# A layer norm's inverse deviations by a power on GpSimd instead of a root on ScalarE, in a cross-attention and mixture-of-experts block

## The chip, the core and the metric

The kernel runs on one core of a Trainium2 chip, in float32. The metric is the device time of one execution in microseconds. A core has five engines that work side by side, each through its own queue in order: TensorE (PE: matmuls and transposes), VectorE (DVE), ScalarE (ACT), GpSimd (POOL), and SyncE (SP), which here only starts transfers.

## The reference

Tokens are x [4, 1024, 256], the context is [4, 64, 256]. With 16 heads of 64 and 8 experts of width 1024, two experts per token:

```python
def _layernorm(x, axis=-1, eps=1e-05):
    m = jnp.mean(x, axis=axis, keepdims=True)
    v = jnp.var(x, axis=axis, keepdims=True)
    return (x - m) / jnp.sqrt(v + eps)

# cross attention, q = layernorm(x), k = v = context
qh = jnp.einsum('bld,hdk->hblk', q, w_qs)
kh = jnp.einsum('bld,hdk->hblk', k, w_ks)
vh = jnp.einsum('bld,hdk->hblk', v, w_vs)
attn = jax.nn.softmax(jnp.einsum('hblk,hbmk->hblm', qh, kh), axis=-1)
out = jnp.einsum('hblm,hbmk->hblk', attn, vh) * qh
out = out.transpose(1, 2, 0, 3).reshape(q.shape[0], q.shape[1], -1)
x1 = x + jnp.tanh(g_xattn[0]) * (out @ w_proj.T + b_proj)

# routed feed-forward on xt = layernorm(x1), top 2 of 8 experts
logits = jnp.einsum('td,ed->te', xt, gate_w)
w_topk, sel = jax.lax.top_k(logits, 2)
w_topk = jax.nn.softmax(w_topk, axis=-1)
combine = zeros((T, E)).at[arange(T)[:, None], sel].add(w_topk)
h = silu(jnp.einsum('td,edf->tef', xt, w1))
y = jnp.einsum('tef,efd->ted', h, w2)
out = x1 + jnp.tanh(g_ffn[0]) * jnp.einsum('ted,te->td', y, combine)
```

There are two norms. The first ("a") feeds the queries, the second ("b") feeds the router and the experts.

## The kernel before

The 4096 tokens are cut into 8 groups of 512; a group is 4 tiles of 128 tokens, and the rows of group g stay on the chip in `xg[g]` (the trace calls these tiles x, buffers x_90 to x_97).

The main loop runs over the groups g and the tiles t of a group. For each tile, `probabilities` makes the scores (L402, the matmuls sc<-keys,qT), takes their maximum over each head's 64 keys (L411, mx), subtracts it (L413, pr<-sc,mx), takes the exp on ACT (L416), sums (L418, sm) and inverts the sum (L419) on DVE, and multiplies on POOL (L421, pr<-pr,sm). `transpose_probabilities` turns the result with PE (L431, pa<-ident,pr) and copies it to aT on ACT (L432). `attend` multiplies with the values (L446, po) and DVE multiplies the result with the query (L455, qT<-po,qT). `project` is L463 (pp<-wp,qT), and L470 adds it to `xg[g]` on DVE. `queries` makes the next group's queries (L387, pq).

The work on routing is one group pair behind: when two groups are finished, `after` is called once for each following tile. Its step 0 calls `ln_stats` for the pair (name "b..."), step 1 `ln_norm` and `logits` for the first of the two groups, step 2 for the second. So the second norm is made four times. For the last pair this comes after the loop, beside the first experts' matmuls.

`ln_stats` gathers mean and variance of each of 8 tiles on DVE (L273 into st, L276 into mv), then makes rstd, the inverse deviations, 128x8 for the pair, in L278 and L279. `ln_norm` subtracts and multiplies tile by tile on DVE (L296). For the second norm it works in place, on `xg[g]`; PE then transposes the tiles (L300, pt_b), ACT copies them (L305, nT_b), and `logits` multiplies with the router's weights (L485, pl<-nT_b,gw), copies on DVE (L493, lT<-pl) and transposes back (L495, pl_t).

`leave` (L1067) stores the finished rows of a group to the output with a DMA from ACT's queue: out_dram<-x. Since the second norm overwrites those rows in place, a normed tile has to wait for the store of its group.

The experts' work comes in slots of 256 or 384 tokens: SP loads weights and rows (L770 to L824), DVE transposes the rows (L836, xT), PE makes the hidden layer (L862, ph<-xT,w), ACT applies silu (L870, hT<-ph), PE makes the output (L987, py), and POOL adds it to the output rows with an indirect DMA (L958, `scatter`). The first slot's hidden layer begins beside the last attention group, the fourth and last pair's norm lies beside the next slots. The small tensors of a slot's tokens (ids) are worked on by DVE in L947 and L950.

Buffers that matter for the order:

- scores have two PSUM buffers (pool ps2): a new one may be written when the subtraction L413 has read the one before the last;
- all other PSUM results (pa, po, pq, pp, pt, pl, and ph until the attention ends) go round four banks (pool ps1);
- the probabilities pr have two buffers in SBUF (pool soft), each free again when its transposes L431 are done.

The order on each engine is set by the tile framework's scheduler at build time, by its own estimates of each operation's cost, within the data dependencies. `behind_softmax` (around L296 for the second norm, and around the scatter) ties an operation to the newest POOL product L421:

```python
newest[:] = [
    nc.gpsimd.tensor_tensor(pr, pr, sm.unsqueeze(2).to_broadcast([P, H, M]), ALU.mult).ins
]
...
def behind_softmax():
    return tc.issue_after(newest[0]) if newest else nullcontext()
```

ACT holds one set of function tables at a time; a function of another set needs a load (ACT_TABLE_LOAD in the trace, LoadActFuncSet in the built order). The root, the exp and the silu each stand in a set of their own here.

Of the kernel before, what the change touches and what calls it, by code (L numbers as in the profile page):

```python
# [8 lines left out]
F32 = mybir.dt.float32  # L9
I32 = mybir.dt.int32  # L10
AF = mybir.ActivationFunctionType
ALU = mybir.AluOpType
# [3 lines left out]
P = 128  # L16
EPS = 1e-5
# [4 lines left out]
def kernel(  # L22
# [36 lines left out]
    nc = tc.nc  # L59
# [26 lines left out]
    const = ctx.enter_context(tc.tile_pool(name="const", bufs=1))  # L86
# [86 lines left out]
    bias = const.tile([P, D], F32, tag="bias", name="bias")  # L173
# [23 lines left out]
        nc.gpsimd.memset(t, 0.0)  # L197
    eps = const.tile([P, 1], F32, tag="eps", name="eps")
    nc.vector.memset(eps, EPS)

    before = const.tile([P, E, E], F32, tag="before", name="before")
    nc.vector.memset(before, 0.0)
# [65 lines left out]
    def ln_stats(groups, name):  # L268
        n = len(groups) * T
        mv = small.tile([P, n, 2], F32, tag="mv", name=f"mv_{name}")  # L270
        for i in range(n):
            st = small.tile([P, 6], F32, tag="st", name=f"st_{name}_{i}")
            first = nc.vector.bn_stats(st, xg[groups[i // T]][:, i % T, :])  # L273
            if i == 0 and name[0] == "a":
                tc.keep_in_program_order(first)
            nc.vector.bn_aggr(mv[:, i, :], st)  # L276
        rstd = small.tile([P, n, 1], F32, tag="rstd", name=f"rstd_{name}")
        nc.scalar.activation(rstd, mv[:, :, 1:2], AF.Sqrt, bias=eps)  # L278
        nc.vector.reciprocal(rstd, rstd)  # L279
        return {g: (mv[:, k * T : (k + 1) * T], rstd[:, k * T : (k + 1) * T]) for k, g in enumerate(groups)}  # L280

    def ln_norm(g, stats, name):
# [762 lines left out]
    ctxT = transposed_context()  # L1045
    pending_keys = keys(ctxT)
    stats = ln_stats([0], "a0")
    next(pending_keys)
    next(pending_keys)
    next(pending_keys)  # L1050
    ln_norm(0, stats, "a")
    next(pending_keys)
    stats = ln_stats(list(range(1, GB)), "a1")
    pending_values = values(ctxT)

# [17 lines left out]
    def after(g, step):  # L1073

        nonlocal entered
        groups = list(range(g - GB + 1, g + 1))
        if step == 0:
            second.update(ln_stats(groups, f"b{g}"))
        elif step == 1:
            second["logits"] = scores_of([R, E], f"lg_{g}")  # L1080
            ln_norm(groups[0], second, "b")
            logits(groups[0], second["logits"])
        elif step == 2:
            for h in groups[1:]:
                ln_norm(h, second, "b")
                logits(h, second["logits"])
        elif step == 3:
            second["routing"] = route(second["logits"], f"{g}")
        if step >= 4:
            if step == 4:  # L1090
                weigh(groups, second["places"])
            first, last = min(6 * (step - 4), 2 * R), min(6 * (step - 3), 2 * R)
            with behind_softmax():
                for i in range(first, last):
                    enter(groups, second["places"], i // R, [i % R])
            entered += last - first
# [130 lines left out]
```

## Time and profile before

| what | us |
|---|---|
| median of 3 runs | 879.75 (878.24 to 880.04) |
| the profiled execution | 878.31 |
| its span | 876.6 |
| PE busy in it | 846.7 |
| DVE, POOL, ACT busy | 452.0, 260.2, 250.6 |

The mean granted clock of TensorE was 0.995 of full speed. PE is the fullest engine: its busy time is close to the span, and the other engines are half idle or more. A long wait of another engine costs nothing unless a matmul stands behind it, so the waits of PE itself are to be read first, then what ended them, stage by stage.

### The profile page before, as it was taken

How to read it: one execution, taken by the hardware profiler on the slowest of the kernel's cores; microseconds unless marked ns; L12 is line 12 of the kernel's file. 1: busy time of each engine (PE TensorE's matmuls, PEld its weight loads, DVE VectorE, ACT ScalarE, POOL GpSimd, SP SyncE). 2: the span in 40 equal slices, each digit the busy share in tenths (PEclk: the TensorE clock that was granted, in tenths of full speed). 3: DMA queues.
4: the chain of work that ended last, by engine and by line, in shares of the span. 5: the costliest groups of instructions: out<-in, count | busy, mean ns of one | idle time of the engine just before them, and what ended most of it. 6: DMA issues, size and time to landing. Idle time of an engine off the chain costs nothing. (4 is left out here: it accounts for less than half of the span.)

```text
span 876.6 us, 13019 instructions
## 1 busy us (share of the span) xinstructions
PE 846.7 (97%) x4632; PEld 665.1 (76%) x4632; DVE 452.0 (52%) x1073; ACT 250.6 (29%) x391; POOL 260.2 (30%) x207
## 2 busy tenths in 40 slices
PE   6999999999999999799999999999999999999995
PEld 4565858576766758587888887777877999999994
DVE  4366484759665975764138212434434445645430
ACT  2574242433342333442032111112121121221210
POOL 3042212113711272205414622222222323133131
PEclk9999999999999999999999999999999999999998
DMA  9999998001200055136675797756481856788421
GB/s 201 338 341 340 341 344 251 25 1 47 75 25 1 25 169 164 49 78 225 185 204 151 192 242 195 192 140 167 93 231 22 236 134 176 181 241 229 114 25 22
DMA packets 163254, 140.56 MB, mean 160 GB/s; under 512 B 72944, under 2 KB 157296, under 8 KB 159344
## 3 DMA queue, kind: packets, MB, share of 16 engines
q1 hardware_dynamic: 143728, 117.84, 46.2%
q0 software_dynamic: 12864, 16.86, 9.9%
q10 hardware_dynamic: 6592, 4.98, 1.8%
q8 instruction: 38, 0.62, 0.3%
q14 instruction: 32, 0.26, 0.1%
HBM read 80.76 MB, written 59.41 MB: 160 GB/s over the span
## 5 line engine op out<-in xcount | busy, mean ns | idle before, releaser
L862 PE MATMUL ph<-xT,w 128*128 128x256 f32 (+1 forms) x960 | 241.9, 408 | 0.1
L862 PEld LDWEIGHTS ph<-xT,w 128*128 128x128 f32 x960 | 180.4, 190 | 50.3 <-issue 1.2
L958 POOL DMA_INDIRECT out_dram<-x,ids x68 | 111.8, 1644 | 312.9 <-DVE x L918 188.1
L870 ACT ACTIVATE hT<-ph 128x1024 f32<-128x1024 f32 (+2 forms) x80 | 71.0, 896 | 271.2 <-PE ph L862 254.2
L421 POOL TENSOR_TENSOR pr<-pr,sm 128x1024 f32<-128x1024 f32 x32 | 61.4, 1918 | 232.4 <-DVE sm L419 169.3
L387 PE MATMUL pq<-nT_a,wq 128*128 128x512 f32 x256 | 116.0, 597 | 7.1 <-DVE qT L455 5.1
L463 PE MATMUL pp<-wp,qT 128*128 128x256 f32 x512 | 113.1, 379 | 0.0
L463 PEld LDWEIGHTS pp<-wp,qT 128*128 128x128 f32 x512 | 97.1, 190 | 18.2 <-issue 5.7
L987 PE MATMUL py<-w,hT 128*128 128x256 f32 x480 | 107.0, 379 | 0.0
L987 PEld LDWEIGHTS py<-w,hT 128*128 128x128 f32 x480 | 90.4, 190 | 12.1
L387 PEld LDWEIGHTS pq<-nT_a,wq 128*128 128x128 f32 x256 | 46.2, 190 | 59.8 <-issue 44.5
L583 POOL DMA_INDIRECT table<-x,to_row x64 | 62.6, 979 | 42.3 <-DVE x L572 21.2
L402 PEld LDWEIGHTS sc<-keys,qT 128*128 128x128 f32 x512 | 62.5, 192 | 11.8 <-issue 11.3
L402 PE MATMUL sc<-keys,qT 128*128 128x128 f32 x512 | 67.0, 278 | 0.0
L432 ACT COPY aT<-pa 128x512 f32<-128x512 f32 x64 | 34.5, 591 | 81.9 <-PE pa L431 71.9
L971 DVE TENSOR_SCALAR x<-py,ids 128x256 f32<-128x256 f32 x30 | 14.5, 482 | 79.4 <-PE py L987 79.3
L908 PE MATMUL q<-sw,sh 128*128 128x128 f32 x456 | 54.0, 275 | 0.0
L411 DVE TENSOR_REDUCE mx<-sc 128x16 f32<-128x1024 f32 x32 | 39.0, 1220 | 26.6 <-PE sc L402 26.4
L908 PEld LDWEIGHTS q<-sw,sh 128*128 128x128 f32 x456 | 52.5, 192 | 0.3
L418 DVE TENSOR_REDUCE sm<-pr 128x16 f32<-128x1024 f32 x32 | 39.0, 1217 | 19.8 <-ACT pr L416 19.8
L394 ACT COPY qT<-pq 128x512 f32<-128x512 f32 x64 | 36.2, 581 | 34.3 <-PE pq L387 34.3
L895 DVE TENSOR_TENSOR sh<-hT 128x512 f32<-128x512 f32 x30 | 20.5, 686 | 48.2 <-ACT hT L870 48.2
(198 smaller groups left out, 873.1 us busy)
## 6 DMA issues: line engine op xcount, KB each, us to landing
w<-in_L_ffn_w_dram SPq DMA_DIRECT2D x60, 1024.0 KB, 6.5
table<-empty SPq DMA_DIRECT2D x8, 4620.0 KB, 36.5
x<-table SPq DMA_DIRECT2D x120, 64.0 KB, 4.5
out_dram<-x ACTq DMA_DIRECT2D x8, 512.0 KB, 7.6
x<-in_x_dram SPq DMA_DIRECT2D x7, 512.0 KB, 9.3
out_dram<-x,ids POOLq DMA_INDIRECT x68, 4.9
wq<-in_L_xattn_w_qs_dram SPq DMA_DIRECT2D x4, 256.0 KB, 5.9
wv<-in_L_xattn_w_vs_dram SPq DMA_DIRECT2D x2, 512.0 KB, 5.9
```

The source lines that it names most:

```text
L387: nc.tensor.matmul(pq, wq[:, c, p * P : (p + 1) * P], nT[g][:, c, :], start=(c == 0), stop=(c == NC - 1),)
L402: nc.tensor.matmul(sc[:, p // 2, :, p % 2, :], of_pair(qT, p)[:, t * P : (t + 1) * P], kT[g // GB][:, p, :], start=True, stop=True,)
L411: nc.vector.tensor_reduce(mx, scv, AX.X, ALU.max)
L418: nc.vector.tensor_reduce(sm, pr, AX.X, ALU.add)
L421: nc.gpsimd.tensor_tensor(pr, pr, sm.unsqueeze(2).to_broadcast([P, H, M]), ALU.mult).ins
L463: nc.tensor.matmul(pp[:, i, :], of_pair(qT, p)[:, t * P : (t + 1) * P], wp[:, p, :], start=(p == 0), stop=(p == NP - 1),)
L583: nc.gpsimd.indirect_dma_start(out=table.rearrange("r (u w) -> (r u) w", w=2), out_offset=bass.IndirectOffsetOnAxis(ap=to_row[:, k, i : i ...
L862: nc.tensor.matmul(ph[:, i, :], a[:, c, f * P : (f + 1) * P], xT[:, c, :], start=(c == 0), stop=(c == NC - 1),)
L870: nc.scalar.activation(hT[f0 // per_tile][:, f1 : f1 + step, :], ph, AF.Silu)
L908: nc.tensor.matmul(to, left[:, f, :], right[:, f, :], start=not onto and f == 0, stop=f == NF // 2 - 1, skip_group_check=onto,)
L958: rows_added = nc.gpsimd.indirect_dma_start(out=outf[:n], out_offset=bass.IndirectOffsetOnAxis(ap=of_rows[:, t, 0, 1:2], axis=0), in_=y[:, t],
L987: nc.tensor.matmul(py[t], hT[f // per_tile][:, f % per_tile, t * P : (t + 1) * P], b[:, f, :], start=(f == 0), stop=(f == NF - 1),)
```

## The change

In `ln_stats`, the second norm no longer takes the root of variance plus eps on ACT and its reciprocal on DVE. It adds eps on DVE and raises the sum to the power −0.5 on POOL, with the exponent from a constant tile broadcast over the 8 columns. The first norm (names that begin with "a") keeps root and reciprocal. Everything behind `rstd` is written as before; what the scheduler does with the new operations is left to it.

```diff
     eps = const.tile([P, 1], F32, tag="eps", name="eps")
     nc.vector.memset(eps, EPS)
+    power = const.tile([P, 1], F32, tag="power", name="power")
+    nc.vector.memset(power, -0.5)
...
         rstd = small.tile([P, n, 1], F32, tag="rstd", name=f"rstd_{name}")
-        nc.scalar.activation(rstd, mv[:, :, 1:2], AF.Sqrt, bias=eps)
-        nc.vector.reciprocal(rstd, rstd)
+        if name[0] == "a":
+            nc.scalar.activation(rstd, mv[:, :, 1:2], AF.Sqrt, bias=eps)
+            nc.vector.reciprocal(rstd, rstd)
+        else:
+            nc.vector.tensor_scalar(rstd, mv[:, :, 1:2], EPS, None, ALU.add)
+            nc.gpsimd.tensor_tensor(rstd, rstd, power.unsqueeze(2).to_broadcast([P, n, 1]), ALU.pow)
         return {g: (mv[:, k * T : (k + 1) * T], rstd[:, k * T : (k + 1) * T]) for k, g in enumerate(groups)}
```

The built order of the changed kernel differs from the one before on these engines (the order itself is a property of the program, not of a run). POOL has the four powers, each directly ahead of the first product L421 of the next tile in the first three places, and between scatters in the fourth. ACT has 10 instructions fewer: four roots and six table loads. On DVE, in the first three places, the first normed tile stands between the maximum L411 and the subtraction L413 of that tile's scores, and the last one of the eight behind the reciprocal L419 of the probability sums in the first two. In the third place the order beside the last attention group also changes: on DVE all eight normed tiles, the index operations L947 and L950, the next maximum L411, the sum L418, the next subtraction L413 and then the reciprocal L419; further on the stream transpose L836 earlier, the third sum L418 ahead of the last four products L455, and the fourth maximum L411 ahead of the copy L493. On PE five of the eight score products of the last tile (each is two matmuls in the trace) stand ahead of the first transposes L431 of that group. In the fourth place the stream transpose L836 stands behind four normed tiles. SP's order is unchanged.

## Prediction

> **What bounds the kernel now.** I read the page first: span, then section 1.
>
> ```profile
> span 876.6 us, 13019 instructions
> PE 846.7 (97%) x4632; PEld 665.1 (76%) x4632; DVE 452.0 (52%) x1073; ACT 250.6 (29%) x391; POOL 260.2 (30%) x207
> ```
>
> PE idles 876.6 − 846.7 = 29.9 us; only what starts a matmul earlier or later counts. The profiled execution took 878.31 us, 1.7 around its span; the median of the runs is 879.75, 1.4 more than it. Next the waits of PE (total, times, longest), and the line view of the root:
>
> ```profile
> PE pa L431 <- POOL pr L421: 5.3, 2, 4.5
> PE pq L387 <- DVE qT L455: 5.1, 6, 1.7
> L278 ACT ACT_TABLE_LOAD  x8: 1283/1283/1283, 3.0 to 443.2; - x8
> L278 ACT ACTIVATE rstd_b<-mv_b,eps x4: 300/300/301, 159.2 to 444.5; 128x8 f32<-128x8 f32 x4
> ```
>
> The second norm is made four times, at 159, 253, 347 and 446 us (stages 1 to 4 below). No wait of PE names it, but one of 4.5 us for the scaled probabilities stands in stage 3. The timeline there (start, us, engine, work, idle before):
>
> ```profile
> 345.61 1.23 DVE L413 TENSOR_TENSOR pr<-sc,mx 128x1024 f32<-128x1024 f32 x1
> 347.67 1.38 DVE L296 TENSOR_SCALAR x<-x,mv_b,rstd_b 128x256 f32<-128x256 f32 x4
> 348.41 3.73 PE L402 MATMUL sc<-keys,qT 128*128 128x128 f32 x32
> 351.04 1.06 DVE L296 TENSOR_SCALAR x<-x,mv_b,rstd_b 128x256 f32<-128x256 f32 x3 [1.98 <-DMA out_dram<-x]
> 352.01 1.21 DVE L418 TENSOR_REDUCE sm<-pr 128x16 f32<-128x1024 f32 x1
> 354.27 0.24 DVE L419 RECIPROCAL sm<-sm 128x16 f32<-128x16 f32 x1
> 354.69 1.90 POOL L421 TENSOR_TENSOR pr<-pr,sm 128x1024 f32<-128x1024 f32 x1 [12.21 <-DVE sm L419]
> ```
>
> The normed tiles overwrite rows that a store (L1067, issued at 343.28) is still reading. DVE therefore stands until 351.04, and the sum, the reciprocal and POOL's product stand behind it; PE's transposes start at 356.64. So a DMA, not the root or its table loads, ends last in stage 3. The stall also costs clock, in the windows view (PE busy is the second column, the granted clock follows POOL):
>
> ```profile
> 352.20:356.60 4.40, 0.00 (x0) 0.00 (x0) 4.40 (x5) 2.15 (x2) 1.90 (x1) 0.98 0.00 0
> 356.60:359.80 3.20, 3.16 (x16) 1.87 (x16) 1.64 (x3) 1.34 (x3) 0.00 (x0) 0.50 0.00 0
> ```
>
> Stage 1's timeline (stage 2 is the same within 0.1 us):
>
> ```profile
> 156.42 1.23 DVE L411 TENSOR_REDUCE mx<-sc 128x16 f32<-128x1024 f32 x1
> 160.85 1.06 ACT L416 ACTIVATE pr<-pr 128x1024 f32<-128x1024 f32 x1
> 163.95 1.90 POOL L421 TENSOR_TENSOR pr<-pr,sm 128x1024 f32<-128x1024 f32 x1 [11.56 <-DVE sm L419]
> 163.96 1.95 PE L402 MATMUL sc<-keys,qT 128*128 128x128 f32 x16
> 165.90 0.33 PE L431 MATMUL pa<-ident,pr 128*128 128x128 f32 x1
> ```
>
> POOL's product ends at 165.85, the scores at 165.9: the transposes start without a wait, with nothing to spare.
>
> **Removed.** Four roots of 0.30 us and, in the built order, six table loads of 1.28 (two each in stages 1, 2 and 4; in stage 3 the silu and exp sets now alternate and the count stays): 1.2 + 7.7 = 8.9 us of ACT, and four DVE reciprocals of 0.20. ACT is busy 29% and ends last nowhere here, so by itself this is worth 0. The Trainium skill, "ScalarE: Activation LUTs", section "What ACT_TABLE_LOAD costs", gives 2.66 us for a switch with its drain; the rows show the root 0.01 us behind its load. Either price lies off PE's path, and the sum is the same.
>
> **Added.** One memset on DVE, under PE's first 4.35 us wait: 0. Four additions on DVE of 128x8, about 0.2 us like the reciprocals they replace: 0. Four powers of 128x8 on POOL, of a length d that no row shows. The nearest rows from below are POOL's copy of 128x4 (0.18 us), from above its product of 128x1024 (1.92) and an indirect store (1.64). A power is many operations on few elements; I take d = 1.0, nearer neither end, and keep 0.2 and 1.9. A loop over single elements could pass the upper end; that is a rival.
>
> **Moved.** In stages 1 to 3 the first normed tile now stands between the maximum and the subtraction on DVE, so DVE waits there for the power, and subtraction, exp, sum, reciprocal and POOL's product queue behind it.
>
> Stage 1, worked out: the addition ends at 156.6, POOL starts 0.17 later (as it does after a reciprocal), so the first tile starts at the later of 157.7 (maximum done) and 156.85 + d. From there: tile 0.33, subtraction 1.14, five tiles 1.63, sum 1.13, tile 0.33, then reciprocal to product 0.42 and product 1.90, together 6.9. With d = 1.0 the product ends at 164.7 instead of 165.85: exp is no longer behind 2.9 us of ACT work, but PE has scores until 165.9. Worth 0. It ends later than 165.9 only if d exceeds 2.1. Stage 2 the same. The store that x_91 waits for is no cover lost: DMA share falls to 0.07 at 158 to 159.
>
> Stage 3: the tiles before the store take 344.75 + d + 2.45 = 348.2, under the wait until 351.04 for any d up to 3.8. Behind 351.04 the new order has four tiles instead of three (1.30), two small index operations (0.14), the second maximum (1.13), the sum (1.13), the second subtraction (1.14), then the reciprocal: at 355.9, against 354.27. Product from 356.3 to 358.2, transposes at 358.25 instead of 356.64: +1.6. In exchange 10 of the 16 matmuls of the fourth scores now stand ahead of the transposes; they need the buffer that the second subtraction frees, at 356.0, and take 2.15 us at half clock, so they fit in the wait. From 356.0 the slow 3.2 us are over at 359.2, the transposes at 359.7, and the third subtraction starts at 359.85 (358.70 before).
>
> What follows is DVE's pace, since `po` and `pt_b` wait for banks that L455 frees: subtraction 1.14, sum 1.13, product 0.59, reciprocal 0.17, three products 1.73, and now a third sum (1.13) where a stream transpose (0.63) stood; the next products start at 365.75 (364.09). The first transposes of the normed rows follow the first of them, at 366.4 (364.80). The work moved forward pays some back, but then the fourth maximum (1.13) stands ahead of the copy lT (L493), which used to come first: scores done at 368.45, maximum to 369.6, copy, `pl_t` at 369.95, and the hidden layer's matmuls at 370.05 instead of 368.55: +1.5. From there on PE is full (its listed waits add up to under 2 us) and nothing gives it back.
>
> Whether PE is slow again after 3.9 us of idleness lies between two rows: 1.72 us at 314 left the clock at 1.00, 4.50 brought it to 0.50. I take the second, being nearer. "TensorE: Matmul & The Clock Gate" (section "Part 1: The HAM clock gate") puts the idle window at about 3.4 us, free-running, which agrees. At full clock the third subtraction would start 0.5 earlier and the sum would be +1.0.
>
> Stage 4: addition at 443.8, power behind scatters that ended at 434; tiles at 444.1 + d, wanted by PE at 452.14: 0 up to d = 6.7. What queues behind the power on POOL starts at 452.
>
> Sum: 0 + 0 + 1.5 + 0 = +1.5, 879.8 for the profiled execution, 881.25 from the median. Its own range is 879.5 to 882.5: +0.9 to +1.9 for the steps, and 0.9 for the spread of the runs.
>
> **Rivals.** First, the slow power (slower): the place is DVE's wait in stages 1 and 2, and it decides from d = 2.1. Each us beyond costs 2 us, one more above 3.8 (stage 3). d = 4 gives +1.5 + 3.8 + 0.2 = 5.5, 885.2; d = 10 would give +27 with stage 4. For it: 8 elements may not be what sets its length. Against: POOL's small rows take 0.1 to 0.3.
>
> Second, the store lands early (faster or level). If it landed by 348.1, as its moving in stages 1 and 2 within 3 us suggests, the second maximum would wait only for its scores at 350.3, and the third subtraction would start at 357.05, 2.8 earlier than in my sum: −1.3, 878.4; with the idle waits around it gone as well, 877.5. Against: the store shares the DMA engines with weight and row loads whose place the change leaves alone (it landed 7.7 us after its issue in stage 3, 7.5 in stage 4).
>
> Third, the new stage 3 order costs nothing visible: the two late chains meet ACT or PE work I have put too early, and 0 remains, 879.75.
>
> **How the numbers follow.** A measurement of this kernel can tell about 0.2% (1.76 us) from no change. My forecast lies just inside, so it is split: chance 0.57, of which 0.33 within and 0.24 slower by more. Slow power 0.25, slower. Early store 0.13, counted as faster though its price is near the bound. No cost 0.05, within. Together faster 0.13, same 0.38, slower 0.49. The range drops the upper part of the slow power (d above 4.5) and the deepest gain: 877.8 to 886.5.
>
> **What would show it.** In the changed profile: the power's row on POOL at 0.2 to 2 us, the first tile's wait for POOL in stages 1 and 2 under 1.3 us, and `pa` at 165.9 and 259.8 without a wait. In stage 3: DVE released by the store at 351.0, the product at 356.3, `pa` at 358.3 behind ten score matmuls at clock 0.50, and a PE wait of about 1.3 us for lT ahead of `pl_t`, which the trace of before has only in the next group (0.41). Wrong: a power over 2.1 us, a release by something other than the store, or the hidden layer's matmuls before 369.5.

## The result and the profile after

The changed kernel took 880.59 us (median of 22 runs, 879.74 to 881.69); in the same series the kernel before took 879.28 (878.24 to 880.60). The ratio is 1.0014, 95% interval 1.0007 to 1.0020: +1.31 us, with an interval of 0.6 to 1.8, inside the 0.2% that was called no difference and slower in sign. The forecast was +1.5, the predicted time 881.2. The profiled execution took 880.54 us around a span of 878.8.

The page after, span and section 1, then the line view of the power (ns minimum/median/maximum, first and last start):

```profile
span 878.8 us, 13010 instructions
PE 846.3 (96%) x4632; PEld 665.7 (76%) x4632; DVE 450.3 (51%) x1074; ACT 242.3 (28%) x381; POOL 266.3 (30%) x211
```

```profile
L285 POOL TENSOR_TENSOR rstd_b<-rstd_b,power x4: 1667/1670/1676, 156.0 to 446.5; 128x8 f32<-128x8 f32 x4
```

ACT lost 8.3 us of work (8.9 were counted) and the time rose all the same. PE's busy time is level (846.3 against 846.7), so the 2.2 us of longer span between the two profiles are idle time of PE (32.5 us against 29.9). The power takes 1.67 us. VectorE's first norm tile waits for it in all four stages, 3.8 us together by the same view, and no wait of PE names it. PE's waits (total, times, longest):

```profile
PE sc L408 <- DVE pr L419: 4.9, 1, 4.9
...
PE pl_t L501 <- DVE lT L499: 1.6, 2, 1.2
...
PE po L452 <- DVE qT L461: 0.7, 1, 0.7
```

Against before, the wait of 4.5 us for POOL's product has become one of 4.9 us for a VectorE subtraction, and two waits are new: 1.2 us ahead of `pl_t` and 0.7 us ahead of `po`. All three stand in stage 3.

Stage 1 after, in the timeline (start, us, engine, work, idle before and its releaser):

```profile
156.01 1.68 POOL L285 TENSOR_TENSOR rstd_b<-rstd_b,power 128x8 f32<-128x8 f32 x1 [4.29 <-DVE rstd_b L284]
157.73 0.41 DVE L302 TENSOR_SCALAR x<-x,mv_b,rstd_b 128x256 f32<-128x256 f32 x1 [0.67 <-POOL rstd_b L285]
...
162.67 1.90 POOL L427 TENSOR_TENSOR pr<-pr,sm 128x1024 f32<-128x1024 f32 x1 [4.97 <-DVE sm L425]
165.08 1.04 PE L437 MATMUL pa<-ident,pr 128*128 128x128 f32 x8
```

The product ends at 164.57 and the transposes start at 165.08 with no wait before them. (From the start-up on, the profile of after runs about 0.7 us ahead of the profile of before; absolute times are compared within one profile below.)

Stage 3 after, PE's timeline:

```profile
347.65 3.73 PE L408 MATMUL sc<-keys,qT 128*128 128x128 f32 x32
356.29 2.48 PE L408 MATMUL sc<-keys,qT 128*128 128x128 f32 x10 [4.91 <-DVE pr L419]
358.56 1.91 PE L437 MATMUL pa<-ident,pr 128*128 128x128 f32 x8
...
363.57 2.98 PE L452 MATMUL po<-aT,vs 64*64 64x512 f32 x16 [0.66 <-DVE qT L461]
...
367.19 0.66 PE L306 MATMUL pt_b<-ident,x 128*128 128x128 f32 x4 [0.23 <-DVE qT L461]
...
370.88 0.33 PE L501 MATMUL pl_t<-ident,lT 128*128 128x128 f32 x1 [1.16 <-DVE lT L499]
371.05 3.62 PE L868 MATMUL ph<-xT,w 128*128 128x256 f32 x16
```

The last line is the start of the hidden layer's matmuls behind the router. Before, it reads:

```profile
368.55 3.62 PE L862 MATMUL ph<-xT,w 128*128 128x256 f32 x16
```

VectorE's timeline after:

```profile
351.24 1.38 DVE L302 TENSOR_SCALAR x<-x,mv_b,rstd_b 128x256 f32<-128x256 f32 x4 [3.24 <-DMA out_dram<-x]
...
356.07 0.24 DVE L425 RECIPROCAL sm<-sm 128x16 f32<-128x16 f32 x1
...
360.57 1.23 DVE L419 TENSOR_TENSOR pr<-sc,mx 128x1024 f32<-128x1024 f32 x1 [2.57 <-PE pa L437]
...
369.41 1.22 DVE L417 TENSOR_REDUCE mx<-sc 128x16 f32<-128x1024 f32 x1 [0.32 <-PE sc L408]
370.55 0.28 DVE L499 COPY lT<-pl 128x128 f32<-128x128 f32 x1
```

The store is still what lets VectorE go (3.24 us of waiting, until 351.24). Behind it come four tiles, the index operations, the second maximum, a sum, the second subtraction and only then the reciprocal at 356.07, as the built order had said. In the windows view (PE busy is the second column, the granted clock follows POOL):

```profile
351.40:356.30 4.90, 0.01 (x1) 0.04 (x1) 4.90 (x11) 1.00 (x3) 0.00 (x0) 0.84 0.01 2
356.30:361.30 5.00, 5.00 (x22) 4.08 (x26) 2.43 (x4) 3.44 (x4) 1.90 (x1) 0.50 0.00 0
```

VectorE is busy for all of the 4.9 us in which PE idles, and then PE works for 5.0 us at half clock, where before it was 3.2.

### The profile page after: what moved, and what is told of

The parts are those of the page before. It is cut to its first block, busy times and chain, and to the rows that moved or that the text cites. A ratio compares the mean times of both kernels' runs of the same rounds, so it can differ in the third digit from the quotient of the medians.

```text
span 878.8 us, 13010 instructions
## 1 busy us (share of the span) xinstructions
PE 846.3 (96%) x4632; PEld 665.7 (76%) x4632; DVE 450.3 (51%) x1074; ACT 242.3 (28%) x381; POOL 266.3 (30%) x211
## 5 line engine op out<-in xcount | busy, mean ns | idle before, releaser
L424 DVE TENSOR_REDUCE sm<-pr 128x16 f32<-128x1024 f32 x32 | 38.9, 1217 | 19.8 <-ACT pr L422 19.8
```

Of the source, the lines that this page charges most:

```text
L424: nc.vector.tensor_reduce(sm, pr, AX.X, ALU.add)
```

## The experiments

Theory A, as the expectations call it: the whole difference comes from stage 3, where VectorE's built order puts more in front of the reciprocal and the copy lT, behind the store; the power (1.67 us) is hidden, and the saved roots and table loads are worth nothing. Its rivals put part of the difference into the power, the other three stages, or some later work. Two questions follow from A: is the store what binds there, and does an order exist that doesn't pay?

To compare runs I use one stretch besides the medians: from the start of the eight-matmul group of `pq` near 314 us to the start of the last `pl` group of the routing pair near 382 us. It holds all of stage 3.

The first four runs were made on another chip, where the kernel before took 896.05 us (median of 35 runs), so only their ratios count.

**Root in stage 3, power elsewhere.**

```
-        if name[0] == "a":
+        if name[0] == "a" or name == "b5":
```

> The third of the four second norms (the pair of groups 4 and 5) keeps root and reciprocal; the other three use the power. In the built order stage 3 is then that of the kernel before on every engine. Theory A (all of the change's cost is the new order of stage 3; power and saved table loads are worth nothing in stages 1, 2 and 4): the time of the kernel before, ratio 1.000 within 0.0005. Theory B (the power's waits on DVE in stages 1 and 2 cost time on PE): between the two kernels or as slow as the change, 879.9 to 880.6 us against 879.3. Theory C (the saved table loads gain, and the order of stage 3 loses more than it seems): faster than before by up to 1 us.

Measured 895.30 us, ratio 0.9996 (0.9985 to 1.0007). With three of the four powers in place and stage 3 in its old order, no loss shows; the interval leaves room for 0.6 us at most.

**Power in stage 3 alone.**

```
-        if name[0] == "a":
+        if name != "b5":
```

> Only the third of the second norms uses the power; the other three keep root and reciprocal. In the built order stage 3 is that of the changed kernel on every engine. Theory A (stage 3's order is the whole cost): as slow as the whole change, +1.3 us on the kernel before (ratio 1.0014 within 0.0007). Theory B (waits in stages 1 and 2): no slower than before. Theory C (table loads gain elsewhere): slower than the whole change, +2 us or more.

Measured 897.92 us, ratio 1.0023 (1.0002 to 1.0044). One power brings the whole cost back, but the interval says little of its size, so the same kernel was run again on a chip where the kernel before takes 879.01 us:

> The power in stage 3 alone, the root in the three other second norms (the kernel of the second experiment, whose interval of 1.0002 to 1.0044 said little of the size). Theory (the whole difference of the two kernels is stage 3's order): 1.0014 against the kernel before, within 0.0008, with a wait of 1.16 us before pl_t. Rival (the powers of the three other stages carry part of it): below 1.0006.

Measured 880.88 against 879.01, ratio 1.0023 (1.0014 to 1.0032). The size is above the 1.0014 that I expected, just past the margin of 0.0008 that I had given it. Nothing is left for the other three powers to carry.

**Norm tiles held behind the reciprocal, with the power.** The tiles that the store holds up are queued, on VectorE, behind the newest reciprocal of a sum:

```
-            with behind_softmax() if name == "b" else nullcontext():
+            with tc.issue_after(inverted[0]) if name == "b" and g % GB else nullcontext():
...
+        inverted[:] = [nc.vector.reciprocal(sm, sm).ins]
```

> The changed kernel, with the normed tiles of the second group of each pair queued on DVE behind the newest reciprocal of probability sums (of the tile that is two later), so that the wait for the store no longer stands ahead of the first sum. Theory A (in stage 3 the store's landing and DVE's order behind it set the start of the transposes): transposes about 2.3 us earlier than in the changed kernel, PE's idle stretch there cut to 1.6 and 1 us with the clock kept at 1.00, and 3 us less in all: 877.5 us, ratio to the kernel before 0.998. Rival (the power or ACT's alternating table loads set it): within 0.5 us of the changed kernel.

Measured 895.32 us, ratio 0.9993 (0.9982 to 1.0003): the gain against the kernel before is about a third of what I expected, and the interval doesn't exclude that there is none. The edit also moves more than the wait: the last tiles and the copy lT now stand ahead of the fourth maximum, and the wait ahead of `pl_t` is 0.42 us instead of 1.16. That exchange alone is worth about 0.7 us (below).

**The same tiles held in the kernel before.** The same edit, on the kernel with the root.

> The kernel before (root everywhere), with the same queueing of the second group's normed tiles. Theory A: the first sum starts at 349.8, when its exp is done, instead of 352.0; transposes at 354.5 instead of 356.6, clock kept at 1.00 behind an idle stretch of 2.4 us instead of 4.5; about 3 us less than before: 876.2 us, ratio 0.9965. Rival (the store is only beside the path, and ACT's root and table loads end last): unchanged within 0.5 us.

Measured 894.54 us, ratio 0.9989 (0.9977 to 1.0001), again about a third, with an interval that touches no gain. Here the scheduler also moved a stream transpose on VectorE and one score product (two matmuls) on PE, so the order beside the last attention group is not quite that of before. VectorE's timelines of these two kernels show why, first the power's, then the root's:

```profile
352.14 0.16 DVE L954 TENSOR_TENSOR ids<-ids 128x2 int32<-128x2 int32 x1 [3.17 <-DMA ids<-table]
```

```profile
350.90 0.17 DVE L948 TENSOR_TENSOR ids<-ids 128x2 int32<-128x2 int32 x1 [2.17 <-DMA ids<-table]
```

Where the tiles had stood waiting for the store, an index operation of 0.16 us now stood waiting for another transfer, the load of its indices. It came 8.64 and 7.95 us after the store's issue, as late as the store itself in the other runs (7.76 to 9.05). The wait had moved to the next instruction in the queue, and the sums behind it began at 353.43 and 351.05, though their exponentials had ended at 351.41 and 349.44. PE still idled 3.55 and 3.87 us.

**The store of that group left out.** The kernel after, without the store of group 5; its rows stay unwritten, and everything else keeps its order on all engines.

```
+        if g == 5:
+            return
```

> The changed kernel without the store of group 5's rows (these rows of the output are left out); the built order is otherwise the same on every engine. Theory A (the landing of this store releases DVE in stage 3): DVE goes on at 348 us instead of 351.2, the second maximum then waits for its scores, the second subtraction frees the score buffer 1.9 to 2.2 us earlier, PE's idle stretch falls from 4.9 to under 3 us, the clock stays at 1.00, and the run is 3 to 4 us shorter than the changed kernel: 876.6 to 877.6. Rival (another release, ACT or POOL, stands right behind): under 1 us shorter.

Measured 878.23 us against 879.54, ratio 0.9985 (0.9975 to 0.9994): 2.4 us less than the 880.59 of the changed kernel in the first series, somewhat less than expected. PE's timeline, then one line of VectorE's:

```profile
354.34 1.35 PE L408 MATMUL sc<-keys,qT 128*128 128x128 f32 x10 [2.08 <-DVE pr L419]
356.47 1.81 PE L437 MATMUL pa<-ident,pr 128*128 128x128 f32 x8 [0.79 <-POOL pr L427]
...
368.69 0.33 PE L501 MATMUL pl_t<-ident,lT 128*128 128x128 f32 x1 [1.16 <-DVE lT L499]
```

```profile
350.57 0.16 DVE L953 TENSOR_TENSOR ids<-ids 128x2 int32<-128x2 int32 x1 [0.40 <-DMA ids<-table]
```

The store is the releaser: without it the long wait falls from 4.91 to 2.08 us. Right behind the tiles VectorE then waits 0.40 us for the index load, the second transfer. (Leaving the store out also takes its traffic away, so this load may have come earlier than with it.) The clock didn't stay at 1.00 as expected: it stood at 0.50 for 3.4 us, from just behind the start of the transposes, which took 1.81 us. The wait ahead of `pl_t` stays at 1.16. It belongs to the order, not to the store.

**The power made twice.** A second power, by one, behind the first:

```
+            nc.gpsimd.tensor_tensor(
+                rstd, rstd, ones[:, 0:1].unsqueeze(2).to_broadcast([P, n, 1]), ALU.pow
+            )
```

> The changed kernel with a second power on POOL behind the first (exponent 1, same shape), so that the tiles wait for 3.3 us of POOL instead of 1.67; the built order is otherwise the same. The prediction put the point from which a longer power costs PE time at 2.1 us in stages 1 and 2, and at 3.8 us in stage 3. Theory A: +1.2 us in stage 1 and in stage 2, 0 in stages 3 and 4: +2.4 us on the changed kernel, 883.0, with a PE wait of about 1.2 us for POOL's product in each of the two. Rival (the power is already on PE's path at 1.67 us): +3.3 us or more. Rival (DVE has more to spare there): 0.

Measured 882.47 us, ratio 1.0034 (1.0022 to 1.0047): 1.9 us more than the changed kernel in the first series, for 2.4 expected. Stage 1, in the timeline:

```profile
158.54 1.64 POOL L286 TENSOR_TENSOR rstd_b<-rstd_b,ones 128x8 f32<-128x8 f32 x1
...
167.11 1.09 PE L440 MATMUL pa<-ident,pr 128*128 128x128 f32 x8 [1.09 <-POOL pr L430]
```

The second power takes 1.64 us and starts 0.07 us after the first ends, so the norm tile behind it comes 1.71 us later; at 3.4 us the power makes PE wait 1.09 us in stage 1 and as much in stage 2. Stage 3's stretch is unchanged (70.11 us against 70.53 and 69.90). From 1.71 later to 1.09 of waiting puts the point from which the power costs at 0.6 above 1.67, or about 2.3 us.

**Both kernels once more**, for the spread between profiled executions.

> The kernel before once more, for a second profile. If the landing of group 5's store varies from execution to execution, the stretch from the pair's statistics to the wait's end in stage 3 differs from the 7.1 us of the first profile, and the hidden layer's matmuls that follow the router's transposes move with it; if it is fixed, it is 7.1 within 0.1.

> The changed kernel once more, for a second profile. In the first, stage 3 took 3.3 us more than in the profile of before, against 1.5 forecast and 1.3 between the medians. If 1 us of it was a late landing of the store and 0.8 a longer stretch at half clock, both of which vary, the second profile shows less than 3.3; if the order alone costs 3.3, it shows 3.3 again and something else in the kernel gains 2.

Measured 878.60 and 879.66 us. In the second profile of before, PE's wait in stage 3 is longer than in either profile of after (4.91 and 4.28):

```profile
356.87 1.97 PE L431 MATMUL pa<-ident,pr 128*128 128x128 f32 x8 [5.79 <-POOL pr L421]
```

The stretch of the second profile of after, 69.90 us, is 2.6 us longer than that of the first of before and 1.2 longer than that of the second. So neither the long wait nor one pair of profiles tells the two kernels apart. What does is the time from the store's landing (the start of the tile it holds up) to the start of the hidden layer's matmuls behind `pl_t`, both read from the timelines:

| kernel | store issued to tile | tile to hidden layer | PE's long wait | stretch |
|---|---|---|---|---|
| before | 7.76 | 17.51 | 4.50 | 67.27 |
| before again | 9.05 | 17.69 | 5.79 | 68.74 |
| root in stage 3 | 8.60 | 17.67 | 5.34 | 68.91 |
| after | 8.72 | 19.81 | 4.91 | 70.53 |
| after again | 8.08 | 19.82 | 4.28 | 69.90 |
| power in stage 3 alone | 8.77 | 19.82 | 4.97 | 71.24 |
| the same again | 8.40 | 19.81 | 4.59 | 70.21 |
| copy before maximum (below) | 8.20 | 19.07 | 4.40 | 69.27 |

The landing varies by 1.3 us from run to run and has the same mean (8.5 us) in both orders, over three and four profiles. Behind it, the new order takes 19.8 us every time and the old one 17.5 to 17.7: 2.2 us that come with the order of instructions. In all four profiles of the new order the clock stood at 0.50 until past the transposes, so what the slow clock adds within the 2.2 us is not separated. In the old order a half clock of 6.8 us instead of 3.4 went with 17.7 instead of 17.5.

**The copy put back ahead of the fourth maximum.** The kernel after, with these two neighbours of VectorE's queue exchanged and nothing else moved on any engine:

```
-        nc.vector.tensor_reduce(mx, scv, AX.X, ALU.max)
+        with tc.issue_after(copied[-2]) if (g, t) == (7, 3) else nullcontext():
+            nc.vector.tensor_reduce(mx, scv, AX.X, ALU.max)
...
+        copied.append(nc.vector.tensor_copy(lT, pl).ins)
```

> The changed kernel with two neighbouring VectorE instructions of stage 3 exchanged and nothing else: the copy lT of the first routing logits stands ahead of the fourth maximum, as in the kernel before, not behind it. Theory (the built order costs its time by several small waits behind the store, of which this is the largest): TensorE's wait before pl_t falls from 1.16 to 0.4 us, and 0.7 us of the 1.3 us between the kernels goes: ratio to the kernel before 1.0004 to 1.001. Rival (the copy is only where a delay shows that the slow clock made earlier, and a wait elsewhere in the stage takes its place): pl_t's wait falls but the stretch from pq to pl stays near 70 us, ratio 1.0012 to 1.002.

Measured 879.55 us against 879.01, ratio 1.0007 (0.9998 to 1.0016).

```profile
369.77 0.33 PE L503 MATMUL pl_t<-ident,lT 128*128 128x128 f32 x1 [0.41 <-DVE lT L501]
```

The wait falls by 0.75 us, the way from landing to hidden layer by 0.74 (19.81 to 19.07). About a third of the 2.2 us is this one exchange of two instructions. The rest of the 2.2 us was not taken apart by runs.

**Tiles and index operations held, with the power.** The two index operations of the first slots are queued behind the reciprocal as well:

```
+        with tc.issue_after(inverted[0]) if inverted and s < NA else nullcontext():
+            nc.vector.tensor_tensor(
+                of_rows[:, :, 0, 1:2], of_rows[:, :, 0, 1:2], of_rows[:, :, 1, 0:1], ALU.min
+            )
...
```

> The changed kernel with two things queued on VectorE behind the newest reciprocal of the probability sums: the norm tiles of the group whose store is under way (as in the run before with the power held), and now also the two small index operations of the first slots, which wait for a load from the routing table. In the run with the tiles alone held, the index operation stood at the head of VectorE until 352.14 and the sums behind it began at 353.43, though their exponential had ended at 351.41. Theory (the store was only the first of two transfers that held VectorE's queue): the first sum starts 1.3 to 1.9 us sooner, the product on GpSimd near 354.4 in place of 356.09 (on that run's time scale), TensorE's wait in stage 3 falls from 3.55 to about 2.0 us, too short for much of the slow clock that followed it (3.0 us at 0.50 to 0.60), and the kernel ends 2 to 3.5 us below the kernel before, a ratio of 0.996 to 0.998. Rival (the sums stand behind the exponential and its table loads on ScalarE, the index operations cost nothing): wait and time as with the tiles alone held, ratio 0.999 to 1.0.

Measured 877.13 us against 879.01, ratio 0.9976 (0.9967 to 0.9985).

```profile
354.53 1.35 PE L409 MATMUL sc<-keys,qT 128*128 128x128 f32 x10 [1.88 <-DVE pr L420]
356.67 1.09 PE L438 MATMUL pa<-ident,pr 128*128 128x128 f32 x8 [0.79 <-POOL pr L428]
```

Against the run with the tiles alone held, only the index operations stand elsewhere; the order on PE, ScalarE and GpSimd is the same.

**The same in the kernel before.**

> The kernel before with the same two things queued behind the reciprocal of sums: norm tiles of the group whose store is under way, and the index operations. With the tiles alone held, the index operation waited until 350.90 for its load, the first sum began at 351.05 although its exponential had ended at 349.44, and TensorE idled 3.87 us with its clock at 0.50 for 6 us after. Theory: sum 1.6 us sooner, TensorE's wait 2.0 to 2.6 us, slow clock for under 3 us; ratio to the kernel before 0.9945 to 0.997 (3 to 5 us less), the fastest of the kernels here. Rival (something else ends last there, the table loads of root, silu and exponential on ScalarE, which stand one behind the other from 345.5 to 353.1): wait 3.5 us or more still, ratio 0.998 to 0.9995.

Measured 875.66 us against 879.01, ratio 0.9963 (0.9949 to 0.9976), the fastest here and faster than both kernels of this study. Against the root kernel with the tiles alone held, again only the index operations moved in this stage; against the kernel before, the other moves named there count too.

```profile
350.30 1.22 DVE L419 TENSOR_REDUCE sm<-pr 128x16 f32<-128x1024 f32 x1 [0.75 <-ACT pr L417]
```

```profile
352.60:354.90 2.30, 0.03 (x1) 0.00 (x0) 2.30 (x4) 2.23 (x3) 1.90 (x1) 1.00 0.00 0
354.90:361.00 6.10, 5.48 (x38) 2.48 (x38) 5.09 (x9) 2.30 (x4) 1.01 (x1) 1.00 0.00 0
```

VectorE's sum now waits 0.75 us for the exponential on ScalarE and no longer for a transfer. PE's wait is 2.30 us (the first window), and the clock stays at 1.00 behind it. In the version with the power it is 1.88 us and the clock stays at 1.00 too. Stage 3 costs 64.5 us in the stretch with the root and 65.8 with the power, against 67.3 to 68.7 in the kernel before: with the waits on transfers gone from both and lT ahead of the fourth maximum in both, the power's order is still the slower one, by 1.3 us.

## Why the prediction was right

**Removed, worth 0.** Right. ACT lost 8.3 us, and the run with three powers and the old stage 3 took the time of before (0.9996).

**The length of the power.** Taken as 1.0 us between bounds of 0.2 and 1.9; it measured 1.67, near the upper row (the product of 128x1024), though it has 8 elements per lane where that has 1024. The nearer row in size was the wrong guide. The 1.0 was a choice between two far bounds, and no row stood behind it. The threshold saved the step: 2.1 us by my sum, 2.3 by the run with two powers.

**Stages 1, 2 and 4, worth 0.** Right, for the reason given: from the first scores to the start of the stretch the two profiles of before take 280.75 and 280.73 us, those of after 280.65 twice. There was less to spare: the product ends 0.51 us ahead of the transposes where I had 1.2, the difference being d. The rival of the slow power had its place and its kind of price right, as the doubled power shows, and fails on the length alone.

**Stage 3, +1.5.** The mechanism is right step by step: release by the store at 351.24 (predicted 351.04), product 5.24 us behind it (predicted 5.26), ten score matmuls ahead of the transposes at clock 0.50, the maximum ahead of lT, a wait of 1.16 us for lT (predicted about 1.3). The term is too small: from landing to hidden layer I had 19.0, the runs have 19.8, against 17.5 before. The shortfall begins with one assumption, that the slow clock would last 3.2 us as before. In the profile of after it lasts 5.3 us from PE's restart (until 361.6). The third subtraction therefore starts 9.33 us behind the landing instead of 8.81; the missing 0.5 us goes on to `pt_b` (15.95 against 15.36), and 0.2 more is lost to the waits ahead of the copy. (This is read from the trace; no run changed the clock alone.) In the medians the step shows as +1.31 (0.6 to 1.8) and, in the kernel with the power in stage 3 alone, as +1.9 (1.2 to 2.8).

Is part of the 2.2 us given back elsewhere? Hardly any, by the traces. From the start of the stretch's last `pl` group to the end, the profiled executions of before take 496.9 and 496.8 us, those of after 496.7 twice; ahead of the stretch the change gains 0.1. What varies is the start-up: the first scores begin at 33.4 and 32.3 us in before, at 32.7 and 32.4 in after. From the first scores to the end, before takes 844.9 and 846.3 us, after 847.8 and 847.2: 1.9 us between the means. That the medians came within 0.2 us of my total is therefore in part luck: the term for stage 3 was some 0.7 us too small. My range of 879.5 to 882.5 also starts 0.25 lower than its own terms give (879.75).

**The early store** came nowhere near its 348.1: in the two profiles of after it landed at 351.24 and 350.31. What its absence is worth (2.4 us against after) is close to the 2.8 that this rival gave. **No cost** is excluded by the interval.

**What I overlooked.** I read the wait on the store as the bound of stage 3. It was only the head of VectorE's queue: the index operation behind it waited for its own load to about the same time. My sum had that operation at 0.14 us, its work alone. That did no harm to the forecast, in which the store came last, but it is why the first two reorderings gave about a third of what I expected of them: with the index operations moved as well, the ratios went from 0.9993 to 0.9976 and from 0.9989 to 0.9963.

## What to carry to other kernels

An engine that works through its queue in order stands at whatever transfer its head waits for. Before pricing a change around such a stall, list every instruction between it and the work that the full engine waits for, and ask of each which transfer it needs: taking away the first waiter alone shows the second. And a change that saves work on an engine with slack, here 8.3 us of ScalarE, is to be judged by the order it leaves on the other engines; here the place of two neighbouring instructions of VectorE alone was worth 0.7 us.

## What the runs showed of the hardware

- **The power on GpSimd.** 128x8 takes 1.67 us and a second one behind it 1.64, nearly the 1.90 of a product of 128x1024 on the same engine. Its length is no matter of scaling by elements from the product.
- **The half clock comes in pieces of 3.4 us.** Summing the windows of half a microsecond, the clock stood at 0.50 around stage 3 for 3.42 us (before), 6.82 (before again), 6.83 (after), 6.82 (after again), 6.83 (power in stage 3 alone), 3.42 (no store), 3.41 (tiles held, power) and 6.83 (tiles held, root). It runs from the fall of the clock, not from PE's restart, which came 0.2 us (before) to 2.6 us (before again) after the fall. What a stall costs in slow matmuls is therefore a matter of phase: 3.2 us of them in one run of the kernel before, 4.3 in the next. The Trainium skill, "TensorE: Matmul & The Clock Gate", section "Part 1: The HAM clock gate", has a free-running window of 3413 ns, and the pieces agree with it.
- **How much idleness it takes.** By the same windows the clock fell 4.3 us after PE had stopped (before), 3.4 and 3.3 (after, after again) and 2.4 (tiles held, root). It stayed at 1.00 through an idle stretch of 2.30 us, and through 1.88 and 0.79 us with 1.35 us of matmuls between; with 2.08 and 0.79 us, without the store, it fell. The same section of the skill lets it fall after an idle window of about 3.4 us; the 2.4 us, and the last case with PE at work in between, show that less can be enough.
- **Another chip.** The kernel before took 896.05 us on one chip and 879 to 880 on the others. The traces of the slower one show waits of PE marked "issue" ahead of `ph` (5.1 us in eight places in one of them). They also show the clock at 0.50 in two more places, beginning between 412 and 417 us and between 497 and 506 us (6.83 us each in the run with the root in stage 3), where no trace from the other chips has it. What brings these about wasn't looked into.
